# A shorter placing of rows, and three steps of attention scores behind each step of the routing

## The chip, the cores and the metric

The kernel runs on one core of one Trainium2 chip. The metric is the device time of one execution in microseconds (us), lower is better. A core has a matrix engine (TensorE, PE in the profile; its weight loads are PEld), a vector engine (VectorE, DVE), a scalar engine (ScalarE, ACT), a general engine (GpSimd, POOL) and one that issues transfers (SyncE, SP). Each works through its own list of instructions in order and waits on semaphores for the others. POOL issues the indirect transfers here.

## The reference

One layer with 8 x 1024 tokens of width 256, all in float32:

```python
xn = layernorm(x)
# attention over the 4 heads of one token (not over tokens)
q, k, v = (xn @ W + b for each)                 # 4 heads of 256
scores  = (q*cos(ph)) . (k*cos(ph)) + (q*sin(ph)) . (k*sin(ph))   # head x head, 4 x 4
s = reshape(softmax(scores / 16) @ v) @ Wo + bo # heads and tokens swapped before the reshape
# experts: 8, two for each token
gates = sinkhorn(xn @ router_w + b, 3 rounds)   # rows, then columns over a batch's tokens
top2, their gates renormalised
e = sum over the two: gate * (relu(xn @ wg) * (xn @ wp)) @ wo
out = x + s * silu(xn + e)
```

## The kernel before

The 8192 tokens are 64 tiles of 128 rows, four tiles to a block (`blk`), 16 blocks. There are four stages, and their instructions are interleaved on purpose.

*Setup and normalising.* Rows are fetched, normalised, turned (`xT`) and written to memory. Logits of the router and bias terms of the scores come into `lg`.

*Routing* (`route`, from L492). A generator with 14 steps, nearly all on VectorE over tiles of 128 x 512: scaled logits, Exp and Ln on ScalarE, maxima and sums over partitions on POOL (`r_cg`, `r_cs`), three rounds of Sinkhorn, the two best experts as flags `hot`. Then `order` (L580) works out the row of a list in which each token's entry goes: a running count `before` of each expert's flags over the free axis (L586, a scan), the counts of the partitions ahead (`count`, `turn`, `within`, `quarter`, `pq`, `prior`), the tiles of 256 rows that each expert gets (`tiles`), which expert owns which tile (`owner`, `first_spare`), and the place `row`. `scatter` (L675) writes the entries with 128 indirect transfers of POOL (L682) in 16 pieces; before each piece a copy to integers, `place` (L679), on VectorE.

*Values' setup* (`setup_values`, L331). The product of the value weights and the output weights, `w_vo`, is formed in 16 groups of matmuls `pw` (L352) with a copy on ScalarE each (L363). These copies are ordered behind the Exp of a routing step: from a given group on behind `shares` (L535), before that behind `first` (L525).

*Attention* (`attention`, L866), a generator which other stages advance by steps with `run(att_gen, n)`. A tile's `score` has nine steps: four chunks of the queries and keys (`py`, L702, copied by ScalarE to `qk`, L709), one with four dot products (L715), and four with a product `kx` (L740) and more dots. The tile `qk` has two buffers. A block ends with two steps of softmax (`soften`). From the second block on, each tile of scores is followed by a step of `value` for the tile four before it: two halves `pu` (L785) with a bias added by VectorE (`u`, L792), then the mixing of the heads, `po_s`. Ahead of the experts the mixing is done by TensorE with a matrix `mixer` (L773, L817); beside the experts VectorE weighs (L804, L808) and TensorE only moves rows (L812). The form is chosen when a tile's value begins.

*Experts* (`experts`, L991). 71 tiles of 256 rows, 68 of them always run. `fetch_entries` reads the list back (L895), `fetch_expert` gathers the rows (`xg`, L908) and loads the expert's weights. `ptr_g` (L933) turns the rows, `pg` and `pp` (L945) and `po` (L961) are the matmuls, and the result is added to `z_d` by an indirect transfer (L974). One or two steps of attention follow each step of an expert. The first turn of an expert's rows is ordered behind the last score that was issued ahead of the experts (`before_experts`).

*The end* reads `z_d` back and forms the output.

What sets the order on each engine: the program is written as a list of instructions, whose order is their priority, and a planner puts into each engine's list the instruction of the highest priority that it thinks to be ready, by its own estimate of durations. `issue_after(x)` adds that an instruction must stand behind `x` on its engine. So the places of `run(att_gen, n)` set priorities; what is late in the planner's view is overtaken. At run time the lists are fixed.

The calls around the change (L1160 on):

```python
for n, _ in enumerate(route(routing, hot, entries)):   # 14 steps
    run(att_gen, 2)
    if n > 2:
        run(values, 1)
...
run(order(routing, prep, hot, keep, placed))
run(values)
put = scatter(entries, placed[0])
next(put)                        # first piece
run(att_gen, 32 - 2 * (n + 1))   # n is 13: 4 steps
for _ in put:                    # 15 pieces
    run(att_gen, 15)
run(att_gen, 13)
```

Of the kernel before, what the change touches and what calls it, by code (L numbers as in the profile page):

```python
# [9 lines left out]
F32 = mybir.dt.float32  # L10
AF = mybir.ActivationFunctionType
ALU = mybir.AluOpType
AX = mybir.AxisListType
# [3 lines left out]
P = 128  # L17
# [13 lines left out]
def recurrent_kernel(  # L31
# [20 lines left out]
    nc = tc.nc  # L52
    B, S, D = x.shape
    H = phase.shape[0]
    E, _, FF = ffn_g.shape
# [3 lines left out]
    R = HD // D  # L59
    J = P // R  # L60
# [6 lines left out]
    G = 256  # L67
# [37 lines left out]
    n = 1  # L105
# [225 lines left out]
    def setup_values(prep, bvT, w_v, w_o):  # L331
# [12 lines left out]
        for i in range(R):  # L344
            for k in range(KD):
                for half in range(2):
                    pw = ps_y.tile([P, 512], F32, tag="y", name=f"pw_{i}_{k}_{half}")
                    for gg in range(2):
                        g = half * 2 + gg
                        for c in range(KD):  # L350
                            with tc.issue_after(newest["logits"].ins):
                                nc.tensor.matmul(  # L352
                                    pw[:, gg * D : (gg + 1) * D],
                                    wvT[g][:, c, k * P : (k + 1) * P],
                                    w_o[i * KD + c],
                                    start=(c == 0),
                                    stop=(c == KD - 1),
                                )

                    done = (i * KD + k) * 2 + half  # L360
                    behind = newest["shares" if done > 4 else "first"]
                    with tc.issue_after(behind.ins) if done > 1 else nullcontext():
                        nc.scalar.copy(w_vo[:, k, i, half * 512 : (half + 1) * 512], pw)  # L363
                yield
        for half in range(2):
            pb = ps_y.tile([P, 512], F32, tag="y", name=f"pb_vo_{half}")
            for gg in range(2):
                cols = slice(gg * D, (gg + 1) * D)
                for i in range(R):
# [4 lines left out]
                        start=True,  # L374
# [202 lines left out]
        yield  # L577


    def order(pool, prep, hot, keep, placed):  # L580
        KT = K * T
        full = [P, E, KT]
        flags = hot.rearrange("p e k t -> p e (k t)")
# [9 lines left out]
        )  # L593
        yield

        count = pool.tile([P, J], F32, name="o_count")
        nc.vector.memset(count, 0.0)
        nc.vector.tensor_copy(count[:, :E], before[:, :, KT - 1])
        turn = [pool.tile([P, J], F32, name=f"o_turn_{n}") for n in range(3)]
        nc.vector.transpose(turn[0], count)  # L600
        now, step = turn[0], 1
        while step < J:
            then = turn[1] if now is not turn[1] else turn[2]
            nc.vector.tensor_copy(then[:, :step], now[:, :step])
            nc.vector.tensor_tensor(
                then[:, step:], now[:, step:], now[:, : J - step], ALU.add
            )
            now, step = then, step * 2
        nc.vector.tensor_tensor(turn[0], now, turn[0], ALU.subtract)
        within = pool.tile([P, J], F32, name="o_within")  # L610
        nc.vector.transpose(within, turn[0])

        quarter = pool.tile([P, R, E], F32, name="o_quarter")
        sums = pool.tile([P, R, E], F32, name="o_sums")
        nc.vector.memset(quarter, 0.0)
        for i in range(R):
            rows = slice(i * J, (i + 1) * J)
            nc.vector.tensor_copy(quarter[rows, i], count[rows, :E])

        pq = ps_gp.tile([P, R * E], F32, tag="gp", name="pq")  # L620
        nc.tensor.matmul(
            pq, ones, quarter.rearrange("p i e -> p (i e)"), start=True, stop=True
        )
        nc.vector.tensor_copy(sums.rearrange("p i e -> p (i e)"), pq)
        total, prior = pool.tile([P, E], F32, name="o_total"), pool.tile([P, E], F32, name="o_prior")
        nc.vector.tensor_reduce(total, sums.rearrange("p i e -> p e i"), AX.X, ALU.add)
        nc.vector.tensor_tensor(
            quarter, sums, below.unsqueeze(2).to_broadcast([P, R, E]), ALU.mult
        )
        nc.vector.tensor_reduce(prior, quarter.rearrange("p i e -> p e i"), AX.X, ALU.add)  # L630
        nc.vector.tensor_tensor(prior, prior, within[:, :E], ALU.add)

        tiles = pool.tile([P, 4, E], F32, name="o_tiles")
        nc.vector.tensor_scalar(
            tiles[:, 0], total, 1.0 / G, 0.5 - 0.5 / G, ALU.mult, ALU.add
        )
        nc.vector.tensor_scalar(tiles[:, 0], tiles[:, 0], ROUND, None, ALU.add)
        nc.vector.tensor_scalar(tiles[:, 0], tiles[:, 0], ROUND, None, ALU.subtract)
        for n, step in enumerate((1, 2, 4)):
            nc.vector.tensor_copy(tiles[:, n + 1, :step], tiles[:, n, :step])  # L640
            nc.vector.tensor_tensor(
                tiles[:, n + 1, step:], tiles[:, n, step:], tiles[:, n, : E - step], ALU.add
            )
        last = tiles[:, 3]
        yield

        col = pool.tile([1, N], F32, name="o_col")
# [8 lines left out]
        nc.vector.tensor_scalar(owner, col, float(E - 1), None, ALU.min)  # L656

        nc.vector.tensor_copy(first_spare, col[:, SURE : SURE + 1])

        base = pool.tile([P, E], F32, name="o_base")  # L660
        nc.vector.tensor_tensor(base, last, tiles[:, 0], ALU.subtract)
        nc.vector.tensor_scalar(base, base, float(G), -1.0, ALU.mult, ALU.add)
        nc.vector.tensor_tensor(base, base, prior, ALU.add)
        pos = keep
        nc.vector.tensor_tensor(pos, before, base.unsqueeze(2).to_broadcast(full), ALU.add)
        nc.vector.tensor_tensor(pos, pos, flags, ALU.mult)
        row = pool.tile([P, KT], F32, name="o_row")
        placed.append(row)
        nc.vector.tensor_reduce(row, pos.rearrange("p e m -> p m e"), AX.X, ALU.add)
        yield  # L670

    def pairs_of(entries):
# [396 lines left out]
    def run(gen, n=None):  # L1069
        done = 0  # L1070
        while (n is None or done < n) and next(gen, StopIteration) is not StopIteration:
            done += 1
# [30 lines left out]
            ALU.add,  # L1103
        )
    nc.vector.tensor_scalar(ids, ids, home, None, ALU.add)

    below = const.tile([P, R], F32, name="below")
    nc.vector.memset(below, 0.0)
    for i in range(1, R):
        nc.vector.memset(below[i * J : (i + 1) * J, :i], 1.0)  # L1110
    with ExitStack() as first_stage:
        prep = first_stage.enter_context(tc.tile_pool(name="prep", bufs=2))
        with tc.tile_pool(name="setup", bufs=1) as setup:
# [34 lines left out]
        with tc.tile_pool(name="routing", bufs=1) as routing:  # L1148
# [3 lines left out]
            for n in range(K):  # L1152
                nc.vector.tensor_copy(pairs_of(entries)[:, n, :, 0], ids)

            keep = prep.tile([P, E, K * T], F32, tag="xT", name="keep", bufs=6)
            nc.vector.memset(keep, 1.0)
            nc.vector.memset(keep[:, :, :1], 0.0)
# [1 line left out]
            values = setup_values(prep, bvT, *fetched_values)  # L1159
            for n, _ in enumerate(route(routing, hot, entries)):  # L1160

                run(att_gen, 2)
                if n > 2:
                    run(values, 1)

# [8 lines left out]
                    tc.declare_no_dep(pad.ins, group="padding", reason="rows behind those copied")  # L1174
                    tc.add_to_no_dep_group("padding", pad.ins)
            placed = []
            run(order(routing, prep, hot, keep, placed))
            run(values)
            put = scatter(entries, placed[0])
            next(put)  # L1180
            run(att_gen, 32 - 2 * (n + 1))
            for _ in put:
                run(att_gen, 15)
            run(att_gen, 13)
    before_experts = newest["score"]
    fin = ctx.enter_context(tc.tile_pool(name="fin", bufs=3))
    wexp = ctx.enter_context(tc.tile_pool(name="wexp", bufs=2))
# [64 lines left out]
```

## Time and profile before

| | |
|---|---|
| Median of 10 runs | 1693.76 us (1690.41 to 1696.71) |
| Profiled execution | 1690.14 us, span 1688.2 us |
| Busy share of the span | PE 96%, DVE 71%, ACT 25%, POOL 38% |
| Routing begins on VectorE (L518) | 85.5 us |
| Scan of `before` (L586) ends | 144.9 us |
| First and last `place` (L679) | 156.6 and 366.6 us |
| First turn of an expert's rows (L933) | 397.3 us |
| Last expert's rows turned (L933, last start) | 1581.2 us |

The profile is one execution, taken by the hardware profiler. A line of the timeline holds start and duration in us, the engine, the source line, the operation, output and inputs, shapes, how often in a row, and in brackets the idle time ahead of it with what ended it. Starts count from the start of the span. Instructions on VectorE overlap a little, so durations are some 0.08 us longer than the distance from start to start. In a table by stretches each engine has its busy time and, in parentheses, its number of instructions.

### The profile page before, as it was taken

The numbers are of one execution on the slowest core, as the hardware profiler recorded it, in microseconds if no ns is written. First come the engines' busy times: TensorE is split into PE (matmuls) and PEld (weight loads), VectorE is DVE, ScalarE is ACT, GpSimd is POOL, SyncE is SP. The second block draws the span as 40 slices with busy tenths as digits, with TensorE's granted clock in tenths as the row PEclk, the third lists the DMA queues.
The fourth block names the chain that finished last, engine by engine and source line by source line (L and its number), as shares of the span: only waits on it lengthen the run. The fifth ranks groups of instructions, "written<-read, shape, count | busy, mean of one in ns | idle before, by whom it ended". The sixth has DMA issues, their size and how long they took to land.

```text
span 1688.2 us, 22808 instructions
## 1 busy us (share of the span) xinstructions
PE 1619.7 (96%) x7669; PEld 994.3 (59%) x7669; DVE 1202.5 (71%) x3689; ACT 427.1 (25%) x807; POOL 637.3 (38%) x599
## 2 busy tenths in 40 slices
PE   6888899999999999999999999999999999999986
PEld 4454344435666666666676666666666666777632
DVE  7779999997675757656666576675766757665776
ACT  4632122222222222222222222212222222222131
POOL 0312756574343443433533333334334433342212
PEclk9999999999999999999999999999999999999998
DMA  9993112122544644644545545445455445555489
GB/s 305 406 360 109 44 59 64 58 67 82 140 117 112 161 106 128 169 106 126 147 105 135 154 130 143 107 128 141 111 149 139 122 116 141 127 127 147 132 272 321
DMA packets 149175, 245.37 MB, mean 145 GB/s; under 512 B 15480, under 2 KB 93600, under 8 KB 148928
## 3 DMA queue, kind: packets, MB, share of 16 engines
q1 hardware_dynamic: 105648, 162.32, 29.4%
q0 software_dynamic: 41376, 77.38, 19.8%
q10 hardware_dynamic: 2032, 4.20, 0.7%
q8 instruction: 62, 1.02, 0.2%
q14 instruction: 57, 0.47, 0.1%
HBM read 176.85 MB, written 75.37 MB: 149 GB/s over the span
## 4 chain that ended last, share of the span: by engine, by line
PE 76%; DVE 15%; DMA 2%; issue 1%; ACT 1%; another core or an unknown queue 1%; POOL 0%; SPq 0%; POOLq 0%; ACTq 0%
PE py L702 23%; PE po L961 13%; PE pg L945 12%; PE pp L945 12%; PE pu L785 11%; DVE junk L715 5%; DVE kx L740 3%; PE po_s L817 2%; DVE w L804 2%; PE ptr_g L933 2%; DMA fz<-z_d 1%; PE po_s L812 1%; DVE u L792 1%; DVE w L808 1%; DVE hid L954 1%
## 5 line engine op out<-in xcount | busy, mean ns | idle before, releaser
L702 PE MATMUL py<-w_qk,xTa 128*128 128x512 f32 x1024 | 476.7, 599 | 9.5 <-ACT qk L709 7.6
L974 POOL DMA_INDIRECT z_d<-y,row x136 | 232.7, 1711 | 666.7 <-ACT y L971 646.1
L715 DVE CUSTOM_DVE_ANT_0 junk<-qk,kx,lg 128x256 f32<-128x256 f32 x768 | 323.5, 480 | 0.2
L702 PEld LDWEIGHTS py<-w_qk,xTa 128*128 128x128 f32 x1024 | 188.8, 191 | 198.2 <-issue 177.3
L715 DVE CUSTOM_DVE_ANT_0 junk<-qk,lg 128x256 f32<-128x256 f32 x256 | 113.9, 481 | 268.5 <-ACT qk L709 268.3
L709 ACT COPY qk<-py 128x512 f32<-128x512 f32 x256 | 149.5, 585 | 473.0 <-PE py L702 440.3
L945 PE MATMUL pg<-xgT,wg 128*128 128x256 f32 x1088 | 264.3, 385 | 0.2
L945 PE MATMUL pp<-xgT,wp 128*128 128x256 f32 x1088 | 260.6, 381 | 0.3 <-DVE hid L954 0.3
L785 PE MATMUL pu<-w_vo,xTa 128*32 128x512 f32 x2048 | 258.7, 599 | 1.8 <-DVE u L792 1.1
L961 PE MATMUL po<-wd,hid 128*128 128x256 f32 x1088 | 257.7, 382 | 0.0
L945 PEld LDWEIGHTS pg<-xgT,wg 128*128 128x128 f32 x1088 | 201.9, 190 | 84.0 <-issue 41.5
L961 PEld LDWEIGHTS po<-wd,hid 128*128 128x128 f32 x1088 | 203.2, 190 | 68.1 <-issue 44.2
L740 DVE TENSOR_TENSOR kx<-qk,mixrow 128x1024 f32<-128x1024 f32 (+1 forms) x256 | 233.8, 952 | 0.0
L945 PEld LDWEIGHTS pp<-xgT,wp 128*128 128x128 f32 x1088 | 204.4, 190 | 39.0 <-ACT hid L953 7.5
L954 DVE TENSOR_TENSOR hid<-pp,hid 128x512 f32<-128x512 f32 x136 | 93.2, 686 | 137.8 <-PE pp L945 127.1
L804 DVE SCALAR_TENSOR_TENSOR w<-u,sc,w 128x256 f32<-128x256 f32 x444 | 185.9, 477 | 1.0
L682 POOL DMA_INDIRECT list_d<-entries,place x128 | 143.3, 1120 | 112.5 <-DVE place L679 78.0
L908 POOL DMA_INDIRECT xg<-xn_d,row x136 | 153.8, 1131 | 54.5 <-issue 44.2
L953 ACT ACTIVATE hid<-pg 128x512 f32<-128x512 f32 x136 | 81.2, 597 | 297.2 <-PE pg L945 271.2
L785 PEld LDWEIGHTS pu<-w_vo,xTa 128*32 128x32 f32 x2048 | 58.8, 109 | 136.6 <-issue 127.8
L971 ACT ACTIVATE y<-po,entry 128x256 f32<-128x256 f32 x136 | 57.1, 470 | 255.9 <-PE po L961 251.3
L792 DVE TENSOR_TENSOR u<-pu,b_vo 128x512 f32<-128x512 f32 x128 | 86.2, 684 | 27.7 <-PE pu L785 27.1
(214 smaller groups left out, 969.7 us busy)
## 6 DMA issues: line engine op xcount, KB each, us to landing
wg<-in_L_ffn_wg_dram SPq DMA_DIRECT2D x68, 512.0 KB
wp<-in_L_ffn_wp_dram SPq DMA_DIRECT2D x68, 512.0 KB
wd<-in_L_ffn_wo_dram SPq DMA_DIRECT2D x68, 512.0 KB
list_d<-empty POOLq DMA_DIRECT2D x1, 9088.0 KB
x<-in_L_attn_x_dram SPq DMA_DIRECT2D x16, 512.0 KB
xn_d<-x POOLq DMA_DIRECT2D x16, 512.0 KB
s_d<-s_out SPq DMA_DIRECT2D x56, 128.0 KB
fo<-in_L_attn_x_dram SPq DMA_DIRECT2D x14, 512.0 KB
```

The source lines that it names most:

```text
L682: put = nc.gpsimd.indirect_dma_start(list_d, bass.IndirectOffsetOnAxis(ap=piece[:, c : c + 1], axis=0), entries[:, at * 2 : at * 2 + LE], ...
L702: newest["score"] = nc.tensor.matmul(py, xT[:, t, k], w[:, k, cols], start=(k == 0), stop=(k == KD - 1),)
L709: nc.scalar.copy(flat[:, cols], py)
L715: newest["dot"] = nc.vector.tensor_tensor_reduce(junk, qk[:, 0, h], k, 1.0 / math.sqrt(D), lg[:, tile_no, E + at : E + at + 1], ALU.mult, ...
L740: nc.vector.tensor_tensor(kx[:, :w], k, mixrow[:, at : at + w].unsqueeze(2).to_broadcast([P, w, 2, D]), ALU.mult,)
L785: nc.tensor.matmul(pu[i * J : (i + 1) * J, :], xT[:, t, k, i * J : (i + 1) * J], w_vo[:, k, i, cols], start=(k == 0), stop=(k == KD - 1),)
L804: nc.vector.scalar_tensor_tensor(w[:, h], part, share, w[:, h], ALU.mult, ALU.add)
L908: nc.gpsimd.indirect_dma_start(xg[:, m], None, xn_d, bass.IndirectOffsetOnAxis(ap=row[:, m : m + 1], axis=0),)
L945: nc.tensor.matmul(dst[:, f], w[:, k, at : at + P], xgT[:, k], start=(k == 0), stop=(k == KD - 1),)
L954: nc.vector.tensor_tensor(h, pp, h, ALU.mult)
L961: nc.tensor.matmul(po[:, m], hid[:, f, m * P : (m + 1) * P], wd[:, f], start=(f == 0), stop=(f == KF - 1),)
L974: add = nc.gpsimd.indirect_dma_start(z_d, bass.IndirectOffsetOnAxis(ap=row[:, m : m + 1], axis=0), y[:, m], None, compute_op=ALU.add,)
```

## The change

Three things are changed.

1. `order` loses the transposes, doubling sums and quarters for the counts of the partitions ahead. Two matmuls take their place: `ones` gives each expert's total, and `above` (1 where the column's number is larger than the partition's) gives the count of the partitions ahead. The sum over the experts' tiles is one scan. The positions are made by eight operations, one for each expert, with a scalar for each partition, and summed by three halving adds, in place of two operations over 1024 columns and a reduce. `owner` and `first_spare` are worked out behind `row`, not ahead of it. The constant `below` goes, `above` comes.
2. Three steps of attention, not two, follow each of the 14 steps of the routing. The steps behind it become 3, 15 times 15, and 2, where they were 4, 15 times 15, and 13. Together that is 272 steps ahead of the experts, where it was 270.
3. The copies to `w_vo` stand behind the Exp of `shares` from the tenth on, not from the sixth.

```diff
-                    behind = newest["shares" if done > 4 else "first"]
+                    behind = newest["shares" if done > 8 else "first"]
                     with tc.issue_after(behind.ins) if done > 1 else nullcontext():
                         nc.scalar.copy(w_vo[:, k, i, half * 512 : (half + 1) * 512], pw)
...
-    def order(pool, prep, hot, keep, placed):
+    def order(pool, prep, hot, keep, above, placed):
...
-        count = pool.tile([P, J], F32, name="o_count")
-        nc.vector.memset(count, 0.0)
-        nc.vector.tensor_copy(count[:, :E], before[:, :, KT - 1])
...
-        nc.vector.transpose(turn[0], count)
-        now, step = turn[0], 1
-        while step < J:
...
-        nc.vector.transpose(within, turn[0])
...
-        for i in range(R):
-            rows = slice(i * J, (i + 1) * J)
-            nc.vector.tensor_copy(quarter[rows, i], count[rows, :E])
...
-        nc.tensor.matmul(
-            pq, ones, quarter.rearrange("p i e -> p (i e)"), start=True, stop=True
-        )
...
+        count = before[:, :, KT - 1]
+        pq = ps_gp.tile([P, 2, E], F32, tag="gp", name="pq")
+        for n, which in enumerate((ones, above)):
+            nc.tensor.matmul(pq[:, n], which, count, start=True, stop=True)
+
+        tiles = pool.tile([P, 2, E], F32, name="o_tiles")
         nc.vector.tensor_scalar(
-            tiles[:, 0], total, 1.0 / G, 0.5 - 0.5 / G, ALU.mult, ALU.add
+            tiles[:, 0], pq[:, 0], 1.0 / G, 0.5 - 0.5 / G, ALU.mult, ALU.add
         )
         nc.vector.tensor_scalar(tiles[:, 0], tiles[:, 0], ROUND, None, ALU.add)
         nc.vector.tensor_scalar(tiles[:, 0], tiles[:, 0], ROUND, None, ALU.subtract)
-        for n, step in enumerate((1, 2, 4)):
...
+        nc.vector.tensor_tensor_scan(
+            tiles[:, 1], ones[:, :E], tiles[:, 0], 0.0, ALU.mult, ALU.add
+        )
+        last = tiles[:, 1]
+
+        base = pool.tile([P, E], F32, name="o_base")
+        nc.vector.tensor_tensor(base, last, tiles[:, 0], ALU.subtract)
+        nc.vector.tensor_scalar(base, base, float(G), -1.0, ALU.mult, ALU.add)
+        nc.vector.tensor_tensor(base, base, pq[:, 1], ALU.add)
+        yield
+        pos = keep
+        for e in range(E):
+            nc.vector.scalar_tensor_tensor(
+                pos[:, e], before[:, e], base[:, e : e + 1], flags[:, e], ALU.add, ALU.mult
+            )
+
+        half = E // 2
+        while half > 1:
+            nc.vector.tensor_tensor(pos[:, :half], pos[:, :half], pos[:, half : 2 * half], ALU.add)
+            half //= 2
+        row = pool.tile([P, KT], F32, name="o_row")
+        placed.append(row)
+        nc.vector.tensor_tensor(row, pos[:, 0], pos[:, 1], ALU.add)
         yield
...
-        nc.vector.tensor_tensor(pos, before, base.unsqueeze(2).to_broadcast(full), ALU.add)
-        nc.vector.tensor_tensor(pos, pos, flags, ALU.mult)
...
-        nc.vector.tensor_reduce(row, pos.rearrange("p e m -> p m e"), AX.X, ALU.add)
         yield
...
-    below = const.tile([P, R], F32, name="below")
-    nc.vector.memset(below, 0.0)
-    for i in range(1, R):
-        nc.vector.memset(below[i * J : (i + 1) * J, :i], 1.0)
...
+            above = routing.tile([P, P], F32, name="above")
+            nc.vector.tensor_scalar(above, column, partition[:, :1], None, ALU.is_gt)
...
-                run(att_gen, 2)
+                run(att_gen, 3)
...
-            run(order(routing, prep, hot, keep, placed))
+            run(order(routing, prep, hot, keep, above, placed))
             run(values)
             put = scatter(entries, placed[0])
             next(put)
-            run(att_gen, 32 - 2 * (n + 1))
+            run(att_gen, 3)
             for _ in put:
                 run(att_gen, 15)
-            run(att_gen, 13)
+            run(att_gen, 2)
```

## The prediction

> **What bounds the kernel now.** I read the page first, for the bound over the whole span; then the busy time by stretches of 20 us, for where that bound is not reached; then who waited for whom in that part; then the timeline at the seam between the two stages.
>
> ```profile
> span 1688.2 us, 22808 instructions
> ...
> PE 1619.7 (96%) x7669; PEld 994.3 (59%) x7669; DVE 1202.5 (71%) x3689; ACT 427.1 (25%) x807; POOL 637.3 (38%) x599
> ```
>
> TensorE (PE) is busy for 1619.7 of 1688.2 us, so it is idle for 68.5 us. Only what shrinks that idle time, or PE's work, can move the end. Stretches of 100 us in the stage of experts show that nothing is to be had there:
>
> ```profile
> 400.00:500.00 100.00, 100.00 (x481) 65.81 (x480) 69.99 (x213) 22.17 (x44) 34.05 (x30) 1.00 0.48 133
> 500.00:600.00 100.00, 99.60 (x477) 66.44 (x476) 65.84 (x192) 23.80 (x46) 37.69 (x35) 1.00 0.49 126
> ```
>
> After the length, the columns are PE, weight loads, VectorE (DVE), ScalarE (ACT), GpSimd (POOL), then granted clock, DMA share and GB/s. From 400 to 1600 us all twelve stretches give PE at least 99.4 of 100. So time won before 400 us passes on to the end one to one. The stage before it, in stretches of 20 us, same columns:
>
> ```profile
> 80.00:100.00 20.00, 18.11 (x65) 11.65 (x66) 15.27 (x49) 7.44 (x11) 1.08 (x2) 1.00 1.11 392
> 100.00:120.00 20.00, 13.12 (x41) 8.98 (x40) 14.95 (x35) 5.80 (x9) 2.15 (x4) 0.83 0.91 330
> 120.00:140.00 20.00, 20.00 (x149) 12.08 (x148) 19.59 (x46) 5.85 (x10) 2.03 (x2) 1.00 0.47 169
> 140.00:160.00 20.00, 14.41 (x32) 6.21 (x30) 19.52 (x70) 4.10 (x7) 2.38 (x3) 0.91 0.12 41
> 160.00:180.00 20.00, 15.43 (x51) 5.07 (x50) 16.46 (x65) 3.08 (x6) 14.97 (x14) 1.00 0.51 168
> 180.00:200.00 20.00, 17.01 (x94) 7.31 (x95) 20.00 (x70) 3.25 (x7) 14.15 (x12) 1.00 0.11 37
> 200.00:220.00 20.00, 20.00 (x88) 9.10 (x90) 20.00 (x74) 5.43 (x11) 15.09 (x14) 1.00 0.23 74
> ```
>
> This is the routing and the placing, where the change lies. From 80 to 200 us PE is idle for 1.9 + 6.9 + 5.6 + 4.6 + 3.0 = 22 us, and VectorE for 4.7 + 5.1 + 0.4 + 0.5 + 3.5 = 14.2 us. The granted clock falls to 0.83 and 0.91 in the two stretches with the long idle of PE: 24 `pw` matmuls behind the first gap take 7.49 us, where 24 ahead of it took 5.34. From 200 us both engines are full: one tile of attention costs 12.5 us on either. With two buffers for `qk`, PE can't be more than two tiles of scores ahead of VectorE. So what VectorE has got through by 200 us decides how early PE runs without a gap.
>
> ```profile
> PE pw L352 <- ACT w_vo L363: 6.9, 1, 6.9
> ...
> PE pq L621 <- DVE o_quarter L618: 5.6, 1, 5.6
> ...
> DVE scm L761 <- ACT sc L759: 3.5, 1, 3.5
> ```
>
> From the waits between 80 and 200 us (total, times, longest): `pw` waits because its copies to `w_vo` stand on ScalarE behind the Exp of `shares`; `pq` waits for the long vector chain of `order`; VectorE waits for an Exp that stands on ScalarE behind copies of scores.
>
> The seam to the experts:
>
> ```profile
> 366.56 0.15 DVE L679 CAST place<-o_row 128x8 int32<-128x8 f32 x1
> 376.90 1.24 POOL L682 DMA_INDIRECT list_d<-entries,place  x1 [0.30 <-issue]
> 380.14 3.63 POOL L895 DMA_DIRECT2D entry<-list_d  x5 [2.00 <-ACT qk L709]
> ...
> 387.30 1.17 POOL L908 DMA_INDIRECT xg<-xn_d,row  x1 [0.30 <-issue]
> 397.31 0.60 PE L933 MATMUL ptr_g<-ident,xg 128*128 128x128 f32 x4
> ```
>
> The last piece of places is ready at 366.56; its scatters, the fetch of the entries and the gather of expert 0's rows follow in a row on POOL, until 388.47. PE turns those rows at 397.31, right behind the last score ahead of the experts, so rows landed by then cost nothing.
>
> **The change part by part.** The steps of attention were counted by walking through the generators.
>
> 1. *Shorter `order`, VectorE work.* From the end of the scan (144.89) to 149.35 VectorE does the cumulative counts, 4.46 us. Of these the change keeps three roundings on 8 columns (0.17, 0.16, 0.17) and adds one scan of 8 columns; the scan of 1024 took 2.27 us, a step on 8 columns 0.15 to 0.17, so I take 0.2. Saved: 3.7, and 0.1 for two memsets at 86.7. The positions took 1.14 + 1.14 + 1.83 = 4.1 us from start to start (L665, L666, L669). In their place come eight scalar_tensor_tensor on 128 columns. Such an instruction takes 477 ns on 256 columns (L804) and 163 on 8 (L419); on the line between them 128 columns take 0.31, so eight take 2.5 (ends 1.3 and 3.8). Three adds follow: 512 columns 0.60 from start to start (L792), 256 columns 0.4 (between 0.68 and 0.28), 128 columns 0.28 (L574). Sum 3.8 for 4.1, saved 0.3. `above` adds 0.28 (a 128x128 compare, L114). The four memsets of `below` were in the setup. Net: -3.8, between -2.5 and -5.0. This lies on the path, since VectorE is full from 140 to 160 and PE waits for it.
>
> [...]
>
> 2. *PE and POOL in `order`.* One matmul on 32 columns becomes two on 8; `pq` on 32 columns took 0.64 us for its two passes, so at most +0.6, in a place where PE is waiting anyway (5.6 us). Without that cover it would cost 0.6. `pq` now waits for the scan alone, not for `o_quarter`: up to 1.3 us earlier (144.89 to 146.2). `owner` is computed behind `row`; it delays the weights of expert 0 (issued at 156.5, used at 399.7) by some 10 us, hidden by 240.
>
> 3. *Three steps behind each step of routing, and `done > 8`.* Tile 2's scores now stand ahead of the third quarter of `pw`, not behind the whole of it, and tiles 3 and half of 4 stand ahead of `order`. Between 104 and 129 us VectorE has no dot to do and waits at each hop. Its waits from 86 to 171 are 2.0 (Exp), 1.4 (Ln), 1.2 (`qk`), 2.0 (Exp), 0.8 + 0.9 + 0.9 (sums over partitions) and 3.5 (Exp of scores): 12.8 us. With four more copies of `w_vo` free of the Exp, the 6.9 us wait of PE should mostly go, and so feed those dots. How much the planned order really fills isn't in the trace: bounds 0 and -12.8. A gain in the middle is nearest to what the rows say, since ScalarE still does everything in order: I take -6.0. Below nothing (a loss) has no row for it here, except through part 5.
>
> 4. *Two steps more ahead of the experts (272, not 270).* The value of tile 18 now begins before the switch and uses the `mixer` form: po_s by L817 takes 1.73 to 1.9 us for eight, by L812 0.57 to 0.64. PE +1.2, nothing hides it. VectorE is spared some 6 us there, worth nothing, as it is at 70%. The tail has the same tiles to do (55 to 63).
>
> 5. *The last place comes later.* Before it stands at step 242 of 270, now at 255 of 272; the last score ahead of the experts is step 266 in both. Places 2 to 15 lie between 180.40 and 366.56, 14.3 us for 15 steps, so 13 steps are 12.4 us. From last place to `ptr_g` there were 30.7 us, now 18.3. The chain through POOL needs 388.47 - 366.56 = 21.9 us and the landing, which is between 0 and the 3.6 us of the entries' fetch. POOL's rows come 3.6 to 7.2 us late for PE. What PE can do meanwhile: the value of tile 18 (32 `pu` 3.6, `po_s` 1.9) and the scores of tile 23 (6.9), 12.4 us, work it does later anyway. If that stands ahead in PE's order, nothing is lost; if not, up to 7.2. The list puts ready work forward (at 397.84 `pu` comes between `ptr_g` and `pg`), so I take +1.5.
>
> Sum: -3.8 - 6.0 + 1.2 + 1.5 = -7.1 us. The profiled execution took 1690.14 us (span 1688.2 and 1.9 around it), so 1683.0. It lies 3.6 under the median of the ten runs, 1693.76; on the median's footing the forecast is 1686.6.
>
> **The rivals.**
>
> *The seam decides (slower).* PE stands idle for expert 0's rows. For it: 18.3 us against at least 21.9, and PE takes its instructions in order. Against: 12.4 us of other work are there. It decides once idle time at the seam is above what parts 1 and 3 bring less 1.2. With 7.2 lost and nothing filled in part 3: -3.8 + 1.2 + 7.2 = +4.6, 1698.4.
>
> *Waits trade places (no change).* VectorE's shorter chain only meets another wait: the `pq` wait and the Exp behind the copies stay, with more dots now ahead of the scan. For it: part 1 is then used up by 1.2 + 1.5 and a little more waiting. -3.8 + 0 + 2.7 = -1.1, 1692.7.
>
> *Both gaps close.* All 12.8 us of VectorE's waits go, and the seam is covered: -3.8 - 12.8 + 1.2 = -15.4; the 2.1 us lost to the lower clock are inside PE's share of that. 1678.4. For it: PE had 22 us idle. Against: eight waits would all have to go.
>
> **How the numbers follow.** Forecast as summed 0.42, both gaps close 0.17, waits trade places 0.14, the seam decides 0.27. A measurement of this kernel can tell about 0.2% (3.4 us) from no change. The forecast's own range is 1681 to 1690. Faster: 0.42 and 0.17 less a little for part 3 at its low end, 0.58. Same: 0.13. Slower: 0.29. The range takes in the two outer cases with the ends of part 1: 1677 to 1700.
>
> **What would show it.** Right: between 100 and 120 us PE has less than 3 us idle and the clock is near 1; `o_row` follows the scan by about 7 us, not 11.3; dots stand between the sums over partitions; from 80 to 200 us PE is idle for 12 us or less. At the seam, `pu` and `py` stand ahead of the first `ptr_g`, and PE has no gap over 2 us. Wrong: a gap of PE ahead of `ptr_g` that ends on the gather of `xg`; a wait of `pq` longer than 5.6; a PE idle time from 80 to 200 that is still near 22.

## The result, and the profile after

The change made the kernel slower: 1706.2 us (median of 9 runs, 1702.33 to 1708.45), against 1693.3 us for the kernel before (30 runs of the same comparison). The ratio is 1.0071, with a 95% interval of 1.0061 to 1.0082. The time is outside the predicted range (1677 to 1700), and the sign was predicted wrong. The profiled execution took 1701.95 us, its span 12.0 us more than before:

```profile
span 1700.2 us, 22768 instructions
...
PE 1625.4 (96%) x7671; PEld 998.3 (59%) x7671; DVE 1190.0 (70%) x3649; ACT 426.6 (25%) x807; POOL 632.6 (37%) x599
```

VectorE has 12.5 us less to do (1202.5 before), and PE idles 74.8 us where it idled 68.5. So time was saved on one engine, and the engine that bounds the kernel waited longer: 6.3 of the 12.0 us are idle time of PE. The other 5.7 us are in PE's busy time, which went up by as much; some of its stretches below run at a lower clock (0.74 to 0.98), and the profile doesn't split those 5.7 us further. The view that located the waits in the prediction, busy time by stretches, for the kernel after (columns: length, PE, weight loads, VectorE, ScalarE, POOL, granted clock, DMA share, GB/s):

```profile
80.00:100.00 20.00, 17.64 (x69) 11.67 (x67) 19.34 (x62) 9.10 (x14) 1.12 (x2) 1.00 1.04 374
100.00:120.00 20.00, 18.92 (x68) 11.04 (x66) 10.76 (x37) 5.93 (x9) 0.00 (x0) 1.00 0.96 351
120.00:140.00 20.00, 18.80 (x145) 11.59 (x146) 17.07 (x39) 6.44 (x13) 4.36 (x5) 1.00 0.41 148
140.00:160.00 20.00, 16.99 (x52) 6.82 (x52) 19.51 (x56) 4.15 (x8) 0.00 (x0) 0.91 0.00 0
160.00:180.00 20.00, 12.22 (x41) 5.55 (x43) 20.00 (x70) 2.10 (x5) 12.15 (x11) 0.74 0.58 191
180.00:200.00 20.00, 13.77 (x74) 5.24 (x66) 16.15 (x54) 1.60 (x4) 14.40 (x14) 0.98 0.14 46
200.00:220.00 20.00, 19.41 (x69) 8.79 (x70) 13.73 (x48) 5.01 (x10) 9.83 (x9) 0.85 0.15 54
...
300.00:320.00 20.00, 17.95 (x70) 7.64 (x69) 18.43 (x67) 4.47 (x8) 8.25 (x9) 1.00 0.16 52
...
380.00:400.00 20.00, 16.59 (x62) 7.31 (x63) 15.28 (x52) 4.33 (x8) 9.00 (x9) 0.91 0.08 27
400.00:420.00 20.00, 12.04 (x56) 5.37 (x55) 11.95 (x39) 1.59 (x4) 15.55 (x22) 0.74 0.19 52
```

Three things are to be seen. The gap of PE at 100 to 120 us is gone (1.1 us idle, 6.9 before). New gaps stand at 160 to 200, where PE had 4.6 and 3.0 us idle and now has 7.8 and 6.2, so that the sum over 80 to 200 us is 21.7 us, as good as unchanged from 22. And at 380 to 420 us PE is idle for 11.4 us where it was full, at a clock of 0.91 and 0.74.

Of the last, the 8.0 us behind 400 are the seam to the experts; the 3.4 us ahead of it are a wait of PE for a copy of `qk` that ends at 383.40. The seam, from the timelines of VectorE, of POOL and of PE, one behind the other:

```profile
390.25 0.17 DVE L654 CAST place<-o_row 128x8 int32<-128x8 f32 x1
...
400.86 0.97 POOL L657 DMA_INDIRECT list_d<-entries,place  x1 [0.30 <-DMA list_d<-entries,place]
403.84 3.63 POOL L870 DMA_DIRECT2D entry<-list_d  x5 [2.01 <-ACT qk L684]
...
408.92 1.12 POOL L883 DMA_INDIRECT xg<-xn_d,row  x1 [0.30 <-issue]
...
402.80 1.92 PE L760 MATMUL pu<-w_vo,xTa 128*32 128x512 f32 x16
411.92 0.45 PE L908 MATMUL ptr_g<-ident,xg 128*128 128x128 f32 x1 [7.20 <-DMA xg<-xn_d,row]
```

The last piece is placed at 390.25 (366.56 before). Its chain through POOL is about as long as before: 21.2 us from the place to the end of the second gather (21.9 before). The first rows are there at 411.92, 21.7 us behind the place; PE stands 7.20 us for them, and 0.76 more for the next. Between the last score ahead of the experts and `ptr_g` PE's list holds 16 `pu` (1.92 us) and nothing else. The other scores and values that could have been done stand behind it. By the way the lists are made, the planner must have taken the rows for ready by then; its own estimate isn't on record.

The gap at 194 to 200 is of another kind. ScalarE and POOL around it:

```profile
197.39 0.97 POOL L657 DMA_INDIRECT list_d<-entries,place  x1 [0.30 <-issue]
...
199.95 1.07 ACT L684 COPY qk<-py 128x512 f32<-128x512 f32 x2 [9.84 <-remote]
```

```profile
190.99 2.84 PE L677 MATMUL py<-w_qk,xTa 128*128 128x512 f32 x6
200.59 5.90 PE L677 MATMUL py<-w_qk,xTa 128*128 128x512 f32 x7 [6.76 <-ACT qk L684]
```

"Remote" means that the profile finds no event of this core that fits the end of the wait. By the lists this copy waits for four `py` of PE; six are on record between 190.99 and 193.83. VectorE's second half of `u`, which waits for PE's `pu` (recorded as done at 191.05), starts at 199.86 after a wait of the same name (3.32 us). Two engines go on within 0.1 us of each other, long after what they wait for seems done, and PE in turn waits 6.76 us for the copy. I call this the standstill.

### The profile page after: what moved, and what is told of

Same layout as the page of the kernel before. It is cut to its first block, busy times and chain, and to the rows that moved or that the text cites. A ratio compares the mean times of both kernels' runs of the same rounds, so it can differ in the third digit from the quotient of the medians.

```text
span 1700.2 us, 22768 instructions
## 1 busy us (share of the span) xinstructions
PE 1625.4 (96%) x7671; PEld 998.3 (59%) x7671; DVE 1190.0 (70%) x3649; ACT 426.6 (25%) x807; POOL 632.6 (37%) x599
## 4 chain that ended last, share of the span: by engine, by line
PE 78%; DVE 10%; issue 4%; POOL 1%; another core or an unknown queue 1%; DMA 1%; ACT 1%; POOLq 0%; ACTq 0%; DVEq 0%; SPq 0%
PE py L677 24%; PE po L936 13%; PE pg L920 13%; PE pp L920 12%; PE pu L760 10%; DVE junk L690 3%; PE po_s L792 2%; DVE kx L715 2%; PE ptr_g L908 2%; DVE w L779 2%; PE po_s L787 1%; PE pw L352 1%; POOL out_dram L1041 1%; DVE w L783 0%
## 5 line engine op out<-in xcount | busy, mean ns | idle before, releaser
L677 PE MATMUL py<-w_qk,xTa 128*128 128x512 f32 x1024 | 481.7, 605 | 20.2 <-ACT qk L684 18.1
L779 DVE SCALAR_TENSOR_TENSOR w<-u,sc,w 128x256 f32<-128x256 f32 x432 | 180.6, 477 | 0.8
L883 POOL DMA_INDIRECT xg<-xn_d,row x136 | 148.5, 1092 | 54.8 <-issue 43.1
```

The lines of the kernel that those rows point to most:

```text
L677: newest["score"] = nc.tensor.matmul(py, xT[:, t, k], w[:, k, cols], start=(k == 0), stop=(k == KD - 1),)
L779: nc.vector.scalar_tensor_tensor(w[:, h], part, share, w[:, h], ALU.mult, ALU.add)
L883: nc.gpsimd.indirect_dma_start(xg[:, m], None, xn_d, bass.IndirectOffsetOnAxis(ap=row[:, m : m + 1], axis=0),)
```

## The experiments

Each kernel computes the whole of the reference. Ratios are to the kernel before, which ran on the same chip between them. The runs fell on four chips, numbered 0, 2, 3 and 6; before took 1691.8 and 1692.8 us on chip 0, 1683.5, 1684.5 and 1684.2 on the others. The chip of the first comparison isn't known; by before's 1693.3 us, and by the waits in its profiles, I take it for chip 0.

### The seam alone, and the last place earlier

*e3*: the kernel before, with its places moved so that the last falls on step 255, as in after.

```diff
-            run(att_gen, 32 - 2 * (n + 1))
+            run(att_gen, 45 - 2 * (n + 1))
...
-            run(att_gen, 13)
```

> The kernel before with the pieces behind the first 13 steps later: 17 steps, not 4, between the first two pieces, and none, not 13, behind the last. The last place stands at step 255 of 270 as in the changed kernel; nothing else differs. Theory A: ptr_g waits for xg for 6 to 9 us, and the ratio is 1.004 to 1.006. Theory B: TensorE's order holds other work ahead of ptr_g and the ratio is within 0.002 of 1.

Measured on chip 2: 1695.09 us, ratio 1.0063 [1.0048, 1.0079]. That is 11.6 us more than before by the medians, 10.6 by the ratio. PE stands idle ahead of `ptr_g`:

```profile
401.48 0.45 PE L933 MATMUL ptr_g<-ident,xg 128*128 128x128 f32 x1 [9.08 <-DMA xg<-xn_d,row]
```

*e1*: after, with the last place 14 steps earlier.

```diff
-                run(att_gen, 15)
-            run(att_gen, 2)
+                run(att_gen, 14)
+            run(att_gen, 17)
```

> The changed kernel, with 14 steps of attention between two pieces of the scatter, not 15, and 17 steps behind the last, not 2. The last place then stands at step 240 of 272, not 255; all else is as changed. Theory A (the seam): the 8.0 us in which TensorE waits ahead of the first ptr_g for xg, and some 2 us of lower clock behind that wait, go; the ratio to the kernel before falls from 1.0071 to between 1.000 and 1.002. Theory B (the loss lies in the routing, and the wait at the seam would only be filled by work that is missing elsewhere): the gap ahead of ptr_g goes, but the ratio stays above 1.005.

Measured on chip 2: 1675.98 us, 0.9954 [0.9939, 0.997]. PE doesn't wait for `xg`, and the first `ptr_g` is at 388.6 us. Together the two settle it: the late last place costs some 10 us, and without it the rest of the change is worth 7.6 us.

### The parts of the change

*e2*: the new `order` alone, with two steps and the copies of before.

```diff
-                    behind = newest["shares" if done > 8 else "first"]
+                    behind = newest["shares" if done > 4 else "first"]
...
-                run(att_gen, 3)
+                run(att_gen, 2)
...
-            run(att_gen, 3)
+            run(att_gen, 4)
             for _ in put:
                 run(att_gen, 15)
-            run(att_gen, 2)
+            run(att_gen, 13)
```

> The kernel before with the new order of the placing alone (two steps behind each routing step, copies of w_vo behind the shares from the sixth on, pieces and steps behind them as before). By the prediction's first part: 3.8 us less, between 2.5 and 5.0, a ratio of 0.997 to 0.9985. Rival: VectorE's saved time turns into another wait, since TensorE's lead of two tiles is set by ScalarE's copies too: ratio 0.999 to 1.001, with TensorE's idle time from 80 to 200 us still near 22.

Measured on chip 2: 1678.69 us, 0.9975 [0.9966, 0.9984], or 4.8 us less than before.

*e4*: e2 with the copies of after (`done > 8`).

```diff
-                    behind = newest["shares" if done > 4 else "first"]
+                    behind = newest["shares" if done > 8 else "first"]
```

> As the run with the new placing alone, and the copies of w_vo stand behind the shares from the tenth on. If the 6.9 us wait of pw is on the path, the ratio is 0.003 to 0.005 below that of the placing alone. If VectorE sets what TensorE gets through by 200 us, the wait of pw goes and another takes its place: the ratio is within 0.001 of that of the placing alone.

Measured on chip 2: 1681.84 us, 0.9985 [0.9974, 0.9995], which is 3.2 us more than e2. Its stretches show the wait of `pw` gone and others in its place:

```profile
100.00:120.00 20.00, 18.90 (x67) 11.49 (x67) 10.08 (x21) 7.38 (x12) 1.42 (x2) 1.00 0.93 339
120.00:140.00 20.00, 13.97 (x104) 6.08 (x106) 19.40 (x51) 2.35 (x4) 2.86 (x3) 0.68 0.41 151
140.00:160.00 20.00, 20.00 (x73) 8.24 (x66) 14.77 (x43) 5.28 (x9) 0.00 (x0) 0.89 0.00 0
160.00:180.00 20.00, 14.20 (x30) 5.49 (x28) 20.00 (x77) 3.50 (x7) 13.30 (x11) 0.91 0.55 190
```

PE is idle for 6.0 and 5.8 us in the second and the fourth line, with the clock at 0.68 and 0.91. The first is a wait for a load, that of the bias `bo_all`:

```profile
130.15 1.07 PE L370 MATMUL pb_vo<-bo_all 1*32 1x256 f32 x8 [6.03 <-DMA bo_all<-in_L_attn_bo_dram]
```

With the wait of `pw` gone, PE comes to this matmul at 124.1 us, ahead of the load; in e2 it comes 7.7 us later and waits 0.59. Behind the wait the 96 matmuls of `pb_vo` take 11.6 us, in e2 6.3. The waits of the fourth line are for copies of `qk`.

*e5*: the old `order` with three steps, `done > 8` and e1's places.

```diff
-                run(att_gen, 2)
+                run(att_gen, 3)
...
-            run(att_gen, 32 - 2 * (n + 1))
+            run(att_gen, 3)
             for _ in put:
-                run(att_gen, 15)
-            run(att_gen, 13)
+                run(att_gen, 14)
+            run(att_gen, 17)
```

> The kernel before with three steps behind each routing step and the copies from the tenth on, the old order of the placing, and the last place early (14 steps between pieces, 17 behind the last, 272 in all). This is part 3 of the prediction with part 4, and without the seam. By the prediction: -6.0 and +1.2, ratio 0.997. By what the profile of the changed kernel shows (the step of the routing behind the first sum over partitions stands behind a dot that waits for scores, VectorE idle for 17 us, not 14): ratio 0.998 to 1.001.

Measured on chip 0: 1727.46 us, 1.0201 [1.0183, 1.0219]. The time is lost behind the routing: POOL's second to fourth scatter took 11.5 us each, 60 more followed without a pause until 296.8 us, and the standstill of VectorE and ScalarE ended at 299.4 and 300.9:

```profile
179.42 11.54 POOL L682 DMA_INDIRECT list_d<-entries,place  x1 [0.30 <-issue]
191.27 11.47 POOL L682 DMA_INDIRECT list_d<-entries,place  x1 [0.30 <-issue]
```

```profile
280.00:300.00 20.00, 0.00 (x0) 0.00 (x0) 0.58 (x1) 0.00 (x0) 12.87 (x14) 0.50 0.14 46
```

PE did nothing at all for 20 us. The run says little of the third step by itself, but much of the standstill.

### After again, and two looks at the routing

*after_again*: after, unchanged, on chip 0.

> The changed kernel once more, unchanged, beside the others of this set. Its profile shows a stall near 195 us in which VectorE, ScalarE and TensorE all stand still for 3 to 7 us with nothing in the lists to wait for. If that stall belongs to the kernel, it is there again at the same place and the ratio is 1.006 to 1.008. If it was a chance of that one execution, the profile has no gap there, and the span is some 6 to 9 us shorter.

Measured: 1705.2 us, 1.0066 [1.0043, 1.0089], with the standstill again (ScalarE's `qk` waits 6.27 us until 197.74).

*e6*: e1 with the copies back at `done > 4`. *e7*: e1 with the dots of tile 2 ordered behind the subtraction of L534. In after, that subtraction stands in VectorE's list behind a dot that ran only at 117.58, while POOL's maximum for it was ready at about 95.

```diff
+            with tc.issue_after(newest["less"].ins) if tile_no == 2 else nullcontext():
                 newest["dot"] = nc.vector.tensor_tensor_reduce(
```

> As the run with places earlier, but the copies of w_vo behind the shares from the sixth on, as before. If done > 8 helps once scores are asked for earlier, this is 0.002 to 0.004 slower than the run with places earlier (0.9954). If it does nothing, or costs 0.001 as it did with two steps, the ratio is 0.994 to 0.996.

> As the run with places earlier, and the dots of tile 2 are ordered on VectorE behind the routing step that follows the first sum over partitions (the subtraction of the columns' maxima), so that this step can't stand behind dots that wait for scores. If that misplaced step is what ate the gain of the three steps, VectorE's idle time from 80 to 200 us falls from 15 to under 8, and the ratio to 0.990 to 0.993. If the copies and matmuls of scores set the pace there, it stays at 0.995.

Measured on chip 0: e6 1689.84 us, 0.9984 [0.9973, 0.9995]; e7 1693.51 us, 1.0009 [0.9999, 1.0018]. Both have a standstill between 179 and 218 us, so their times can't be read against e1's on chip 2. Against e1's later run on chip 0 (1691.39 us, below), e6 is 1.6 us faster and e7 2.1 us slower, and the runs of all three overlap: as far as the standstills let it be read, the later copies show no gain with three steps. In e7 VectorE idles 20.3 us from 80 to 200 us, not under 8, and PE has 4.95 of 20 us busy at 160 to 180, where it waits 14.2 us for `qk`: the wait has moved. My theory that this subtraction was the place where part 3 lost its gain has fallen.

### The standstill: kernel, or chip?

Until here five profiles showed it (after, after again, e5, e6 and e7), the last four of them taken on chip 0, and four on chip 2 didn't. Four kernels were run on one chip: after; e1; *e8*, which is e1 with the first two pieces set apart; and *e9*, which is e8's idea with two steps (15, 14 and 17).

```diff
             next(put)
-            run(att_gen, 3)
+            run(att_gen, 13)
             for _ in put:
-                run(att_gen, 14)
-            run(att_gen, 17)
+                run(att_gen, 13)
+            run(att_gen, 22)
```

> The kernel after, unchanged, beside three kernels with other places. Two things cost it time by the runs so far: the seam (PE idle ahead of the first ptr_g, priced 10.7 us by the run that only placed pieces later) and the standstill of ACT and DVE near 195 us (PE idle about 7 us, and a clock of .85 behind it), which was seen in five profiles of one chip and in none of four on another. If the standstill comes of the kernel: 1.007 again. If it comes of the chip, and this is the other chip: only the seam is left of it, ratio near 1.002 (the 0.9954 of the run that placed earlier, plus 10.7 us).

> After, with the last piece placed 14 steps earlier, unchanged from its first run (0.9954 there, no standstill, 48 scatters of POOL in a row). If the standstill near 195 us comes of POOL's scatters in a row whatever the chip: it must show now or have shown then, so a second run without it (ratio 0.995, PE over 17 of 20 us busy in 180 to 200 us) speaks against that. If it comes of the chip: on the chip where it was seen before, ratio near 0.999 with ACT's copy of qk waiting over 6 us between 185 and 220 us; on the other, 0.995.

> The same as the run beside it (three steps, shorter order, last piece at nearly the same step), but 13 steps between the first two pieces, not 3, so that POOL has a pause between its 16 scatters of one piece and the next. If POOL's scatters in a row make the standstill: none here, ACT's waits on qk under 3 us each in 180 to 220 us, ratio 0.995 on any chip, 4 to 7 us ahead of the run beside it where that one has the standstill. If the chip makes it whatever POOL does: the standstill stays and both are equal within 0.1%.

> The shorter order and the later copies, with two steps behind each of the routing, 15 steps between the first two pieces, 14 between the others and 17 behind the last. Against the run beside it with three steps and the same pause it tells what the third step is worth by itself. My theory, that the waits only trade places: within 0.15% of it, ratio 0.995 to 0.997. The theory of the forecast, that the third step saves up to 6 us: 0.35% behind it, ratio 0.998 to 0.999.

Measured, chip 0 once more: after 1707.22 us, 1.0098 [1.007, 1.0125]; e1 1691.39, 0.9995 [0.9981, 1.0009]; e8 1683.43, 0.9952 [0.9937, 0.9967]; e9 1689.89, 0.9986 [0.9975, 0.9997]. The stretches around 200 us of e1, then of e8:

```profile
180.00:200.00 20.00, 16.65 (x90) 6.43 (x88) 19.54 (x69) 1.92 (x4) 15.52 (x14) 0.97 0.15 48
200.00:220.00 20.00, 17.03 (x61) 7.18 (x62) 12.92 (x43) 3.88 (x7) 11.19 (x11) 0.91 0.19 64
```

```profile
180.00:200.00 20.00, 19.95 (x98) 7.90 (x97) 19.20 (x67) 4.15 (x8) 12.41 (x13) 0.99 0.12 40
200.00:220.00 20.00, 20.00 (x102) 8.66 (x101) 20.00 (x74) 4.04 (x9) 13.88 (x13) 1.00 0.32 93
```

In e1 POOL issues 32 scatters without a pause (168.4 to 213.1 us), in e8 16, then 8 after a pause. On the chip with the standstill, setting the pieces apart takes this one away (short waits of 1.6 and 2.3 us are left there) and is worth 8.0 us. The third step is worth 6.5 us (e8 against e9), so the theory that its waits only trade places has fallen too. But e9 has a wait of 4.9 us for `bo_all`, as e4 has, and e8 none, so part of the 6.5 us can be this wait.

The next four fell on chip 6. *e10* is after with its late last place, but with the pieces apart; *e11* has the old `order` and e8's steps.

```diff
             next(put)
-            run(att_gen, 3)
+            run(att_gen, 17)
             for _ in put:
-                run(att_gen, 15)
-            run(att_gen, 2)
+                run(att_gen, 14)
+            run(att_gen, 3)
```

> After, with 17 steps between the first two pieces instead of 3 and 14 between the others, the last piece placed at the same step as in after (255). If two independent things cost the kernel after its time: the standstill near 195 us is gone (PE over 19 of 20 us busy in 180 to 200 us), the seam is still there (PE idle 6 to 11 us ahead of the first ptr_g), and the ratio is that of the run with the places apart and early (0.9952) plus the seam's 10.7 us: 1.0005 to 1.0025. If the standstill were only another place for the same lost time: 1.006 or more.

> The longer order of before, with three steps, the later copies, and the places apart as in the run beside it. Told apart: what the shorter order is worth with three steps. By the run of the order alone (4.2 us) this is 0.25% behind the run beside it, ratio 0.9975 to 0.9985, and the 1.0201 of the same kernel with the first two pieces 3 steps apart was the standstill alone, 20 us and more of it. If three steps with the longer order lose time by themselves: over 1.005, with PE idle in 200 to 300 us.

> Shorter order, three steps, places apart and early, unchanged from its first run (0.9952). No standstill again, ratio 0.994 to 0.997. Were it a matter of chance, and not of the places, a standstill shows and the ratio is 0.998 or more.

> The shorter order alone, two steps, the first two pieces 4 steps apart, unchanged from its run on another chip (0.9975, no standstill, PE 18 to 20 of 20 us busy in 180 to 220 us). If the standstill takes only pieces placed closely on a chip that shows it: PE idle 5 us or more in 180 to 220 us here, ratio 0.999 to 1.001. If it takes the third step as well: no standstill, 0.9975.

Measured: e10 1685.45 us, 1.0009 [1.0, 1.0019]; e11 1692.59, 1.005 [1.0033, 1.0067]; e8 1675.92, 0.995 [0.9932, 0.9968]; e2 1679.46, 0.9973 [0.9963, 0.9984]. None has a wait called remote in this part, not even e2 with 32 scatters in a row. So e10 less e8, 9.5 us, is the seam by itself. e11 was expected at 0.9975 to 0.9985: in it four of the second to fifth scatters take 11.55, 6.40, 4.83 and 11.55 us, POOL never catches up, and the seam opens though the last piece is placed early (PE 13.20 of 20 us in 380 to 400). Why POOL's scatters are so long with the old `order` and three steps wasn't found.

The last two fell on chip 3.

> The kernel after, unchanged. Three runs of it on one chip gave 1.007 to 1.010 with the standstill in each profile; two other chips have shown no standstill in seven profiles of other kernels. If the chip decides on the standstill and this is another chip: only the seam is left, ratio 1.000 to 1.003 (the 0.9954 of the run with earlier places, on such a chip, plus the seam's 9.5 to 10.7 us), PE over 19 of 20 us busy in 180 to 220 us. If the kernel decides: 1.007 or more anywhere.

> The shorter order and the later copies, two steps, places apart and early. On the chip with standstills it was 0.9986 where three steps gave 0.9952. If the third step is worth that anywhere: 0.9975 to 0.999 on another chip too, where three steps gave 0.9950. If the difference was a matter of that chip: 0.995 to 0.9965.

Measured: after 1686.04 us, 1.0009 [0.9998, 1.0019]; e9 1683.28, 0.9992 [0.998, 1.0005]. After's stretches on this chip:

```profile
180.00:200.00 20.00, 20.00 (x102) 8.75 (x94) 20.00 (x73) 4.05 (x8) 15.43 (x16) 1.00 0.14 46
200.00:220.00 20.00, 20.00 (x98) 8.17 (x98) 20.00 (x70) 4.10 (x9) 15.73 (x15) 1.00 0.33 103
380.00:400.00 20.00, 11.97 (x43) 5.25 (x41) 15.87 (x54) 3.31 (x6) 15.29 (x20) 0.86 0.15 42
```

The standstill is gone and the seam is there as before (8.0 us idle in the last line). That is the change without what chip 0 adds: 1.5 us slower by the medians, with an interval from 0.3 us faster to 3.2 us slower. e9 is again 0.4% behind e8 (0.9992 here, 0.995 on chip 6), with 3.8 us of waiting for `bo_all`.

The profile of before, on which the prediction was made, has such a wait too. POOL and ScalarE there:

```profile
376.90 1.24 POOL L682 DMA_INDIRECT list_d<-entries,place  x1 [0.30 <-issue]
...
379.04 1.07 ACT L709 COPY qk<-py 128x512 f32<-128x512 f32 x2 [9.44 <-remote]
```

It costs PE 3.5 us in 360 to 380 (16.50 of 20 busy). The profiles of before and after that the comparison began with, and the eight others taken on chip 0, all have such waits between 150 and 410 us; the ten others, on chips 2, 3 and 6, have none. In all ten the last run of 16 scatters without a pause is followed, 0.8 to 1.0 us after its end, by the end of such a wait (378.14 and 379.04 above; 381.83 and 382.77 in after). Near 195 us it is otherwise: there after's first profile has the end of a run at 198.36, 1.5 us ahead of the end of its waits, but in the five others with a standstill there (after twice more, e1, e6 and e7) waits of 6.3 to 15.1 us end at 194 to 201, in the midst of a run of 24 to 32 scatters that goes on until 202 to 217. On the other chips runs of 16 to 128 scatters have no such wait in them or behind them. So the waits are seen beside POOL's runs of scatters on that chip, and that spacing two pieces takes one of them away was shown. The cause is open: that signals of PE come late there is a reading of the records, not shown. Not every long run has one, and in one place (e8 at 296.14, 6.48 us) it comes at the end of a run of 8.

## Why the prediction was wrong, point by point

The steps against what was measured, in us of the medians:

| Step of the prediction | Predicted | Measured |
|---|---|---|
| 1, shorter `order` | -3.8 | -4.8 (e2, chip 2), -4.7 (e2 again, chip 6) |
| 3 and 4, three steps, later copies, two steps more | -6.0 + 1.2 = -4.8 | -2.7 (e1 less e2, chip 2), -3.5 (e8 less e2, chip 6) |
| 5, last place later | +1.5 | +9.5 (e10 less e8, chip 6), +11.6 (e3 less before, chip 2) |
| Sum of the steps | -7.1 | +1.5, between -0.3 and +3.2 (after on chip 3) |
| Not in the prediction: the standstills of chip 0 | 0 | some 11 |

**Step 5 failed, and with it the sign.** It has three terms, and two of them were wrong. The chain through POOL was right: 21.9 us from the place to the end of the second gather, 21.2 now. The first wrong term is the 18.3 us that PE would be busy between the last place and `ptr_g`. It comes from the 30.7 us of before, and these hold a wait:

```profile
379.68 3.70 PE L702 MATMUL py<-w_qk,xTa 128*128 128x512 f32 x8 [3.50 <-ACT qk L709]
```

In e2, which doesn't have it, the same way is 27.2 us (360.36 to 387.58). With the last place late, the work up to the last score takes 12.6 us in after (390.25 to 402.80) and 12.3 in e3 (380.13 to 392.40). So the rows come 9.1 us behind the last score, not 3.6 to 7.2. The second wrong term is the 12.4 us of other work that would stand ahead of `ptr_g`: 1.92 us did in after, none in e3, which waited 9.08 + 0.82. That after's wait of 7.20 + 0.76 is near the prediction's "up to 7.2" is luck: 1.92 us of cover make up for most of the first error. The prediction took an instruction behind `ptr_g` in before's list (`pu` at 397.84) for proof that the list moves ready work forward; but what stands behind `ptr_g` covers nothing ahead of it. A smaller part of the price lies beyond the idle time (e3 lost 10.6 to 11.6 us with 9.9 idle, e10 9.5 with 8.1): after the wait PE runs at a clock of 0.74 (400 to 420 us), and 16 `pu` take 2.82 us there, where 16 ahead of the wait took 1.92. The rival of the seam named this place and priced it at 7.2 us; it measured 9.5.

**Step 1 was right** with two steps, 1 us under what it brought and within its ends; with three its worth wasn't measured cleanly (e11). The eight operations on 128 columns took 2.17 us (2.5 assumed); the adds 0.60, 0.34 and 0.21 from start to start (e8). That these shapes would not lose the part was right too: the positions take 3.3 us in all, where 3.8 was predicted and before has 4.1.

**Step 2 was right.** `pq` waits 3.0 us in after, 5.6 in before.

**Step 3: the size was near, the mechanism was not.** The prediction let the gain come from the 6.9 us wait of `pw`, with the third step feeding VectorE. By the runs the copies alone bring a loss, +3.2 (e4 less e2): the wait of `pw` goes, and PE comes too early to the load of `bo_all` (6.0 us, and a clock of 0.68) and waits for `qk`. The third step, with the two steps more of step 4, brings -5.9 (e1 less e4, chip 2) or -6.5 (e9 to e8, chip 0). With it PE comes to that load at 135.0 us (e1) and doesn't wait; with two steps and the later copies it waits 3.8 to 6.0 us (e4 and e9 twice). How much of the gain is that, and how much anything else, wasn't told apart. That VectorE is fed better isn't seen: from 80 to 200 us it idles 15.2 us in after on chip 3, where before has 14.2. Together the copies and the third step leave -2.7 to -3.5.

**Step 4** can be read from the stage of experts. Where neither kernel waits in it, it lasts 1184 us from the first `ptr_g` to the last with 270 steps (387.2 to 1571.4 in e2) and 1180 with 272 (388.6 to 1568.6 in e1): the value of tile 18 moved out of it, as said. Its own price wasn't measured apart.

**The sum.** With 9.5 in the place of 1.5 the prediction's steps give +0.9 us, and the change on a chip without standstills measured +1.5. The other 11 us of the 12.9 in the result I put to the standstills of chip 0 and what they bring with them: in after's profile PE is idle for 6.8 us in the first, 2.1 in the one at 300 to 320 and 3.4 in the one at 380 to 400, where before has only the 3.5 at 360 to 380. That is 8.8 us more, and the clock of 0.85 behind the first (19.41 us of PE at 0.85) is worth some 2.9, an estimate. No step or rival had this. The sign of it was in the profile of before, a `qk` wait of 9.44 us without a releaser, and I read past it.

**The signs.** PE's idle time at 100 to 120 us below 3 and a clock near 1: so it came. `o_row` 7 us behind the scan: it ends 9.6 us behind it (154.42 to 164.03), because dots stand in between. PE idle 12 us or less in 80 to 200: it is 21.7 with the standstill and 14.4 without (after on chip 3). A gap ahead of `ptr_g` that ends on `xg` was named as the mark of a wrong prediction, and it is there.

**What beats both.** e8, the change with the last place early and the pieces apart, takes 0.9952 and 0.995 of the time of before on two chips.

## What to carry to other kernels

When a change moves the start of a long chain (21.2 us through POOL in after), look up in the consumer's fixed list what really stands ahead of the waiting instruction; work that exists but stands behind it covered nothing here (PE waited 7.20 us in after, 9.08 in e3). And a stretch of time in a profile is only work once its waits are taken out. A wait that went, such as that of `pw`, has to be followed to the next wait before its time is counted. And before a result is explained, run the same kernel on another chip: here the same two kernels differ by 0.1% on one and by 0.7 to 1.0% on another.

## What of the hardware was not expected

One chip of four ran before some 8 us slower (1691.8 and 1692.8 against 1683.5 to 1684.5 us), and there engines stand for up to 15.1 us (e6; 35.6 us in e5) at waits whose cause the profile shows as done, in part long before. Those behind the last run of 16 indirect transfers end 0.8 to 1.0 us behind it; those near 195 us mostly end in the midst of a run. A single scatter of 128 entries on POOL, 0.96 us at its best, took 11.5 us in two kernels on two chips (e5 and e11). Beside the first of these in e11, from 178 to 188 us, VectorE's instructions are nearly all the same dots and products as in e8, where the scatters take 0.96 to 1.97 us. What makes the long ones long wasn't found.
